# RGCN layer with a highway gate on one core: node orders at one visit, adding transfers behind the slot gathers, one branch flag, thin slots between full ones

## The chip, the cores and the metric

The kernel runs on one core of one Trainium2 chip. The metric is the device time of one execution in microseconds (us). The core's engines each have their own stream of instructions: TensorE (PE, matrix products; its loads of weights are listed as PEld), VectorE (DVE), ScalarE (ACT), GpSimd (POOL) and SyncE (SP). SP and POOL issue most transfers; the transfers themselves run on 16 DMA engines that all queues share. In the profile, queue q1 holds the transfers that SP issues and q0 those that POOL issues.

## The reference

The input is x of 1250 nodes by 1024 features, 20000 edges (src, dst, type), eight 1024 x 1024 relation matrices, a root matrix and a gate matrix of 2048 x 1024. All is fp32.

```python
h = relu(layernorm(x))
u = h @ root + bias
for r in range(8):
    mask = (edge_type == r)
    sums = segment_sum(h[src] * mask[:, None], dst)
    cnt = segment_sum(mask, dst)
    u = u + (sums / maximum(cnt, 1)[:, None]) @ weight[r]
z = concat([u, h], axis=1) @ w_gate + b_gate
out = x + (tanh(u) * z + h * (1 - z))
```

The mean over the edges of a relation and the product with its matrix may be exchanged: the kernel first forms y[r] = h @ weight[r] for all nodes, and then, for each destination node, adds rows of y with weight 1/cnt.

## The kernel before

**The steps.** PE works through eleven products in a row, called steps s = 0 to 10: seven of the relations and one before them, the root, the lower half of the gate matrix (applied to h) and last its upper half (applied to u). Nodes are cut into ND = 10 blocks of 128 (the last 98), which are taken in five pairs. Steps 1 to 9 save multiplications by a two-level scheme after Strassen and Winograd: each step has seven *kinds* n = 0 to 6, and (s, n) names one of them. A kind has five *calls* in which PE runs the products of one pair of blocks; between two calls a hook lets other work put its instructions into the streams. Where the text says "at (2,2), call 2" it means that hook. Steps 0 and 10 go by pairs of blocks, so (10, i) is pair i of the last step. Within a kind, PE's matmuls are the lines L330 and L337 (L589 in the last step), DVE adds to banks of partial sums (L438 in the first half of a kind, L461 near its end, L388, L381 and L382 for what goes to rows), ACT copies banks (L424, L448, L344 and others), DVE forms the next right factors (L238) and left factors (L276 to L286). Some left factors are loaded back from memory instead: L296, `w<-lefts_dram`, 512 KB each, issued by SP about twelve us before PE needs them.

**The order.** The kernel schedules itself by hand: what stands in an engine's stream is the order of the Python statements, and the generators below (`yield`) are moved on by one part at each call. So work beside the products lands at a fixed place in each engine's stream, and an engine that waits for one of its instructions holds up all that follows in its stream.

**The index part**, beside steps 0 to 2. It sorts the edges. Relations are taken in G = 3 groups (0 to 2, 3 to 5, 6 and 7). Within a group the nodes are ordered by how many edges they have, so block 0 of the order holds those with the most; K says how many slots (edges per node) each block needs: 21, 10, 8, 7, 7, 6, 5, 5, 4, 3 for groups 0 and 1, and 17, 7, 6, 5, 4, 4, 3, 3, 2, 2 for group 2. `nodes_in_order(g)` does ten one-hot matmuls (L804) from operands that DVE builds (L787 to L798), turns the result into node numbers, and issues ten gathers (helper `rows_of`, L728) of the edge lists, `idx<-table`, on POOL. It is called for groups 0, 1 and 2 at call 2 of (2,1), (2,2) and (2,3). Behind the gathers of each group stand 3, 3 and 4 adding transfers (L1237), `out<-h_dram` with accumulation, 512 KB each: the reference's `out = x + h + ...`. `counts(g)` (L769 to L774) counts the edges of each node and relation; `weights(g)` (L757 to L764) turns counts into `w_of`.

**The first branch.** If some node has more edges than the tables hold, `counts_over` does a long repair. It loads the flag `n_far` into a register on five engines and stands before step (3,0); all that is left of `counts` is done right before it. With these inputs the branch isn't taken, and each engine jumps over the body (some 280 instructions on DVE, 1400 on POOL, about 50 on the others).

**The groups.** From BEGIN = (3,1), `edges(g, ...)` goes through the slots of group g, one *visit* each: `add_slot` issues on POOL one gather of up to 128 rows of y (L1407, `got<-y,idx`, five buffers, 512 KB when all rows are in range; rows out of range move nothing) and has DVE multiply and add it (L1412) to the block's `u`. The visits are spread over the calls, 76 slots from (3,1) to (6,1) and from (6,1) to (8,5), and 53 from there on. `starts` and `leaves` give for each block the first visit and the one at which its `u` is done; groups 0 and 1 write `u` back to memory, and group 2 adds the root product (`hr_dram`) and goes on to the gate, where ACT takes tanh of it (L1857) and PE transposes it (L533).

**The second branch** stands after group 1: if nodes have more edges than K gives them slots, the remaining edges are added in a long body. Its flag `n_pass` comes from `passes_needed` (30 row maxima of `w_of`, L1498, and a chain of small operations, among them a transposition on PE). Before it stand `rest()` and `store_rows()`, which add and store the last rows of the step (L381, L382). It skips some 1220 instructions on DVE, 2060 on POOL, about 30 on ACT and PE.

**The last step.** `make_t1` to `make_t4` (L202, L206, L210, L214) form sums of the gate's right factors. `product` takes its pieces in the order of its small functions `p1()` to `p7()`; `p2` is the piece with A12.

## Time and profile before

| what | us |
|---|---|
| median of 3 runs | 1289.93 (1285.99 to 1290.58) |
| the profiled execution | 1283.34 |
| its span, first to last instruction | 1281.5 |
| PE busy | 1249.9 |
| DVE busy | 970.8 |
| POOL busy | 443.7 |
| ACT busy | 274.4 |
| mean granted clock of PE | 0.996 |

A row of the timeline has the start in us, the busy time, the engine, the line, the operation, output and inputs, the count, and in brackets the idle time before it with what ended it ("DVEq" is DVE's own sequencer, which includes branches). A row of the windows has the stretch, the busy time of each engine with the number of instructions, the granted clock, the share of the DMA engines in use and GB/s. Times are from the span's start.

### The profile page before, as it was taken

The numbers are of one execution on the slowest core, as the hardware profiler recorded it, in microseconds if no ns is written. First come the engines' busy times: TensorE is split into PE (matmuls) and PEld (weight loads), VectorE is DVE, ScalarE is ACT, GpSimd is POOL, SyncE is SP. The second block draws the span as 40 slices with busy tenths as digits, with TensorE's granted clock in tenths as the row PEclk, the third lists the DMA queues.
The fourth block names the chain that finished last, engine by engine and source line by source line (L and its number), as shares of the span: only waits on it lengthen the run. The fifth ranks groups of instructions, "written<-read, shape, count | busy, mean of one in ns | idle before, by whom it ended". The sixth has DMA issues, their size and how long they took to land.

```text
span 1281.5 us, 14045 instructions
## 1 busy us (share of the span) xinstructions
PE 1249.9 (98%) x4725; PEld 883.1 (69%) x4725; DVE 970.8 (76%) x1462; ACT 274.4 (21%) x517; POOL 443.7 (35%) x400
## 2 busy tenths in 40 slices
PE   9999999899989999999999999999999999999996
PEld 5444777677767777777777777777777777544443
DVE  7545898786579787887878779898888799766642
ACT  3452211121122112112111211211221121202210
POOL 1330000028202222322431333453442558854531
PEclk9999999999999999999999999999999999999999
DMA  7965445838946686898898768899995949999973
GB/s 303 195 191 163 156 149 195 242 107 211 294 149 224 205 280 222 321 335 305 287 341 281 251 197 294 294 331 352 365 301 204 349 141 342 346 333 228 234 150 57
DMA packets 130432, 317.87 MB, mean 248 GB/s; under 512 B 30999, under 2 KB 32222, under 8 KB 130190
## 3 DMA queue, kind: packets, MB, share of 16 engines
q1 hardware_dynamic: 85726, 186.64, 42.7%
q0 software_dynamic: 44336, 129.72, 34.3%
q8 instruction: 38, 0.62, 0.2%
q10 hardware_dynamic: 288, 0.52, 0.1%
q14 instruction: 44, 0.36, 0.1%
HBM read 258.79 MB, written 90.18 MB: 272 GB/s over the span
## 4 chain that ended last, share of the span: by engine, by line
PE 43%; issue 10%; DMA 7%; POOL 7%; DVE 2%; POOLq 0%; ACT 0%; DVEq 0%; SPq 0%; ACTq 0%
PE ps_n L330 14%; PE ps L330 14%; PE ps_b L337 9%; DMA got<-y,idx 5%; PE ps_q L330 4%; POOL got L1407 3%; DMA z_dram<-w 2%; PE ps_b L589 1%; POOL h_all L728 1%; POOL out_dram L739 1%; POOL u L728 1%; PE ps_n L589 1%; POOL w L728 0%; DVE h_all L1412 0%; DVE u L1412 0%
## 5 line engine op out<-in xcount | busy, mean ns | idle before, releaser
L1407 POOL DMA_INDIRECT got<-y,idx x205 | 256.0, 1249 | 435.5 <-DVE u L1412 332.6
L330 PE MATMUL ps<-w,h_all 128*128 128x256 f32 (+1 forms) x1040 | 258.7, 392 | 0.0
L1412 DVE SCALAR_TENSOR_TENSOR u<-got,w_of,u 128x1024 f32<-128x1024 f32 (+1 forms) x189 | 241.5, 1280 | 12.4 <-DMA got<-y,idx 9.8
L330 PE MATMUL ps_n<-w,w 128*128 128x256 f32 x976 | 234.2, 383 | 9.2 <-DVE ps L438 7.3
L330 PEld LDWEIGHTS ps_n<-w,w 128*128 128x128 f32 x976 | 185.0, 191 | 63.2 <-issue 22.2
L337 PE MATMUL ps_b<-w,h_all 128*128 128x512 f32 x504 | 226.6, 592 | 0.0
L330 PEld LDWEIGHTS ps<-w,h_all 128*128 128x128 f32 x1040 | 197.4, 190 | 39.6 <-issue 14.1
L337 PEld LDWEIGHTS ps_b<-w,h_all 128*128 128x128 f32 x504 | 95.8, 190 | 94.1 <-issue 90.9
L589 PE MATMUL ps_b<-w,h_all 128*128 128x512 f32 x312 | 139.4, 593 | 4.4 <-DVE w L206 2.6
L330 PE MATMUL ps_q<-w,w 128*128 128x256 f32 x488 | 116.8, 383 | 5.4 <-DMA w<-lefts_dram 5.4
L448 ACT COPY ps<-ps_n 128x512 f32<-128x512 f32 x122 | 64.8, 575 | 252.5 <-PE ps_n L330 209.1
L330 PE MATMUL ps<-w,w 128*128 128x256 f32 x488 | 115.6, 380 | 0.0
L330 PE MATMUL ps_n<-w,h_all 128*128 128x256 f32 x488 | 115.3, 379 | 0.0
L589 PEld LDWEIGHTS ps_b<-w,h_all 128*128 128x128 f32 x312 | 58.6, 190 | 77.4 <-issue 73.0
L438 DVE TENSOR_TENSOR ps<-ps_n,inner 128x256 f32<-128x256 f32 x122 | 50.5, 430 | 75.0 <-PE ps L330 67.8
L330 PEld LDWEIGHTS ps_q<-w,w 128*128 128x128 f32 x488 | 93.1, 191 | 19.4 <-DVE w L388 4.8
L330 PEld LDWEIGHTS ps<-w,w 128*128 128x128 f32 x488 | 93.1, 191 | 12.8
L330 PEld LDWEIGHTS ps_n<-w,h_all 128*128 128x128 f32 x488 | 92.7, 190 | 13.0 <-issue 0.5
L424 ACT COPY ps<-ps_n 128x256 f32<-128x256 f32 x122 | 39.7, 361 | 247.0 <-PE ps_n L330 178.6
L238 DVE TENSOR_TENSOR w<-w,w 128x2048 f32<-128x2048 f32 x36 | 82.3, 2287 | 0.3
L589 PE MATMUL ps<-w,h_all 128*128 128x512 f32 (+1 forms) x136 | 57.6, 567 | 0.0
L728 POOL DMA_INDIRECT idx<-table,node_key x30 | 32.5, 1082 | 58.6 <-DVE small L788 47.9
(247 smaller groups left out, 1154.8 us busy)
## 6 DMA issues: line engine op xcount, KB each, us to landing
w<-lefts_dram SPq DMA_DIRECT2D x102, 512.0 KB
w<-in_L_gnn_weight_dram SPq DMA_DIRECT2D x31, 1024.0 KB
y<-row SPq DMA_DIRECT2D x84, 256.0 KB
y<-w SPq DMA_DIRECT2D x42, 256.0 KB
w<-in_L_gnn_w_gate_dram SPq DMA_DIRECT2D x8, 1024.0 KB
lefts_dram<-w SPq DMA_DIRECT2D x14, 512.0 KB
h_dram<-h_all SPq DMA_DIRECT2D x9, 512.0 KB
y<-row SPq DMA_DIRECT2D x9, 512.0 KB
```

Of the source, the lines that this page charges most:

```text
L238: nc.vector.tensor_sub(w[to], w[a], w[b])
L330: nc.tensor.matmul(p, a[:, k], b[:, k], start=(fresh and k == 0), stop=(k == a.shape[1] - 1), skip_group_check=True)
L337: nc.tensor.matmul(to, h_op[NP - 1][:, ORDER[n], k], w[:, k], start=(fresh and k == 0), stop=(k == KQ - 1), skip_group_check=True)
L424: nc.scalar.copy(banks[2 * u][:, :H], xs[u])
L438: nc.vector.tensor_add(banks[2 * u][:, H:], xs[u], ys[:, u * H:(u + 1) * H])
L448: nc.scalar.copy(banks[2 * u + 1].rearrange("p (a n) -> p a n", a=2), xs[u][:, None, :].to_broadcast([P, 2, H]))
L589: nc.tensor.matmul(b[:, at], aop[:, i, k, :], w.of[i][:, k, at], start=(fresh and k == 0), stop=(k == KQ - 1), skip_group_check=True)
L728: nc.gpsimd.indirect_dma_start(out=to, out_offset=None, in_=of, in_offset=bass.IndirectOffsetOnAxis(ap=at, axis=0), compute_op=op)
L739: ins = nc.gpsimd.indirect_dma_start(out=of, out_offset=bass.IndirectOffsetOnAxis(ap=at, axis=0), in_=frm, in_offset=None, compute_op=op)
L1407: nc.gpsimd.indirect_dma_start(out=t[:n], out_offset=None, in_=y[g][:, :], in_offset=bass.IndirectOffsetOnAxis(ap=at[:n, d, k:k + 1], axis=0),
L1412: nc.vector.scalar_tensor_tensor(u[:n], t[:n], w, u[:n], op0=OP.mult, op1=OP.add)
```

## The change

- **Node orders.** `nodes_in_order` handles all three groups at one visit, call 2 of (2,2): the operands are built before it in parts, in separate tiles for each group, then thirty one-hot matmuls and thirty gathers in a row.
- **Adding transfers.** The ten L1237 transfers move into `beside_group` and stand on POOL behind all thirty gathers.
- **Counts.** `counts(0)` comes at (2,4), `counts(1)` and `counts(2)` at (2,5); each of them earlier in the program than step (3,0).
- **One flag.** `beyond()` finds from `idx` whether any block's next slot is in use, with a few comparisons for the blocks that share a K, and joins the answer with the other flag before the existing `any_over`, now at call 2 of (2,6). `passes_needed` and `n_pass` go. The register `far` serves both branches, so the second branch doesn't load one.
- **Branches.** The first now stands after (3,0), before (3,1); the second isn't preceded by `rest()` and `store_rows()`. Both get `preferred_fallthrough_block=False`: the path not taken falls into a short block that jumps over the body.
- **Slots.** Block 0's slots above K of block 1 (eleven in groups 0 and 1, ten in group 2, the thin ones) are put between the slots of the later blocks, one behind each of the first three of every four of these. Before, they came right after block 0's other slots. Block 0 of groups 0 and 1 now leaves at visit 43 instead of 29, of group 2 at 37 instead of 24.
- **Last steps.** `make_t1` moves to (5,3), `make_t2` to (6,1), `make_t3` to (6,2) of step 9, with other homes for t1 and t2; in a kind that is done in the regular way, part of the rows is put one call earlier; in the last `product`, `p2()` comes before `p7()`.

The tiles `pool_of`, `kpos`, `mid`, `found` and `held` are only allocated earlier, and `at` in `edges` lists the (block, slot) of each visit.

```diff
+    BESIDE = (4, 3)
...
-                self.place = dict(b11=old["a"], t3=old["e"], b22=old["b"], t1=old["d"],
-                                  t2=rights, b21=lefts, t4=old["c"])
+                self.place = dict(b11=old["a"], t3=old["e"], b22=old["b"], t1=rights,
+                                  t2=old["d"], b21=lefts, t4=old["c"])
...
+                if i == 3:
+                    to_rows_of(1, (0,))
...
-            to_rows_of(1)
+            to_rows_of(1, (2,))
...
+        elif (n, k) == (5, 3):
+            gate.make_t1()
         elif (n, k) == (6, 1):
-            gate.make_t1()
+            gate.make_t2()
         elif (n, k) == (6, 2):
-            gate.make_t2()
-        elif (n, k) == (6, 3):
             gate.make_t3()
...
         else:
+            p2()
             d = p7()
             last(d, 0)
             p3()
...
-    def nodes_in_order(g, pos, ids_f, a, b, small, many):
+    def nodes_in_order(pos, ids_f, room, many):
+        parts = []
+        for g in range(G):
+            a, b, small = room(g)
...
+            yield
...
+            parts.append((a, b, lo_f))
         while at_call[2] != 2:
             yield
-        p = sum_bank("ps_q")
-        for c in range(ND):
-            nc.tensor.matmul(p[:, :2 * ND], a[:, c], b[:, c], start=(c == 0), stop=(c == ND - 1))
...
-        for d in range(ND):
-            rows_of(idx[:, g, d, :], table_rows, node_key[:, g, d:d + 1])
+        p = sum_bank("ps_q")[:, :2 * G * ND].rearrange("p (g d) -> p g d", g=G)
+        for g, (a, b, lo_f) in enumerate(parts):
+            for c in range(ND):
+                nc.tensor.matmul(p[:, g], a[:, c], b[:, c], start=(c == 0), stop=(c == ND - 1))
...
+        for g in range(G):
+            for d in range(ND):
+                rows_of(idx[:, g, d, :], table_rows, node_key[:, g, d:d + 1])
+            yield
...
-                for g in range(G):
-                    yield from nodes_in_order(g, pos[:, g * ND:(g + 1) * ND], ids_f, junk, hot, room, many)
-                    assert not xh
-                    for d in range(g * ND // G, (g + 1) * ND // G):
-                        nc.gpsimd.dma_start(out[block(d)], h_dram[block(d)], accum_op=OP.add,
-                                            max_dma_last_dim=4 * D)
...
+                yield from nodes_in_order(pos, ids_f, room, many)
...
-            starts = [late + sum(K[g][:d]) for d in range(ND + 1)]
-            leaves = [starts[d + 1] - 1 + lag for d in blocks]
+            full = K[g][1]
+            thin = [(0, k) for k in range(full, K[g][0])]
+            at = [(0, k) for k in range(full)]
+            for j, a in enumerate((d, k) for d in blocks[1:] for k in range(K[g][d])):
+                at.append(a)
+                if j % BESIDE[0] < BESIDE[1] and thin:
+                    at.append(thin.pop(0))
+            starts = [late + at.index((d, 0)) for d in blocks]
+            leaves = [late + at.index((d, K[g][d] - 1)) + lag for d in blocks]
...
-        def passes_needed():
-            far_k = got()[:, :NHI]
-            nc.vector.memset(far_k, 0.0)
-            for g in range(G):
-                for d in range(ND):
-                    if K[g][d] < SLOTS:
-                        nc.vector.reduce_max(far_k[:, g * ND + d:g * ND + d + 1],
-                                             w_of[:, g, d, K[g][d]:], axis=AX.X)
...
         def beside_group():
-            yield
+            added = iter(range(ND))
+            def add_h():
+                for d in added:
+                    nc.gpsimd.dma_start(out[block(d)], h_dram[block(d)], accum_op=OP.add,
+                                        max_dma_last_dim=4 * D)
+                    return
             for g in range(G):
-                yield from counts(g)
+                for _ in range(3):
+                    yield
+                for _ in counts(g):
+                    add_h()
+                add_h()
+            yield
+            yield from beyond()
+            while at_call[2] != 2:
                 yield
+            any_over()
...
+        def beyond():
+            flags = const.tile([P, NHI], F32, name="flags")
...
+                    nc.vector.tensor_single_scalar(
+                        flags[:, used:used + n].rearrange("p (g d) -> p g d", d=e - d),
+                        idx[:, gs[0]:gs[-1] + 1, d:e, k], float(FAR), op=OP.is_lt)
...
+            nc.vector.reduce_max(most[:, 1:2], flags, axis=AX.X)
+            nc.vector.tensor_max(most[:, 2:3], most[:, 2:3], most[:, 1:2])
...
-            if (s, i) == (BEGIN[0], BEGIN[1] - 1):
-                for _ in ready:
-                    pass
-                counts_over()
-                ready = weights_of_groups()
+        assert next(ready, 0) == 0
+        far = load(n_far)
+        counts_over(far)
+        ready = weights_of_groups()
...
-        rest()
-        store_rows()
-        passes = nc.values_load(n_pass[0:1, 0:1], min_val=0, max_val=E // MORE,
-                                skip_runtime_bounds_check_because="no more passes than edges")
-        with tc.If(passes > 0):
+        with tc.If(far > 0, preferred_fallthrough_block=False):
```

More of the change, by code (lines that the diff above doesn't have):

```diff
@@ L1444, in edges @@
             for t in range(-1, leaves[-1] + 4):
-                for d in blocks:
-                    if starts[d] <= t < starts[d + 1]:
-                        add_slot(u[d], g, d, t - starts[d], idx[:, g], w_of[:, g])
+                if late <= t < late + len(at):
+                    d, k = at[t - late]
+                    add_slot(u[d], g, d, k, idx[:, g], w_of[:, g])
                 for d in blocks:
@@ L1746, in tile_rgcn_highway @@
             s, i = beside(group, sum(K[g]) + late + 1, s, i, CHANGE[g])
[L1749 to L1753 removed]
+        with tc.If(far > 0, preferred_fallthrough_block=False):
             def further(g, d, ks, at, w):
@@ L1768, in tile_rgcn_highway @@
                         further(g, d, range(K[g][d], SLOTS), idx[:, g], w_of[:, g])
-            over = nc.values_load(n_over[0:1, 0:1], min_val=0, max_val=E // MORE,
-                                  skip_runtime_bounds_check_because="no more passes than edges")
+            over = load(n_over)
             with tc.If(over > 0):
```

113 lines of the change are left out of this document (52 added, 61 removed).

## The prediction

> **What bounds the kernel now.** The page first: it says which engine fills the span.
>
> ```profile
> span 1281.5 us, 14045 instructions
> PE 1249.9 (98%) x4725; PEld 883.1 (69%) x4725; DVE 970.8 (76%) x1462; ACT 274.4 (21%) x517; POOL 443.7 (35%) x400
> ```
>
> TensorE (PE) is busy 98% of the span, so an edit pays only where it lets PE wait less. The change leaves PE's matmuls as they are in number and size. What can be won is the 31.6 us (1281.5 - 1249.9) in which PE stands still. The waits say who stood for whom: in total us, how often, the longest (four rows of PE, two of VectorE, DVE, for later):
>
> ```profile
> PE ps_n L330 <- DVE ps L438: 7.3, 4, 4.7
> PE ps_q L330 <- DMA w<-lefts_dram: 5.4, 3, 4.5
> PE ps_b L589 <- DVE w L206: 2.6, 1, 2.6
> PE ps_b L589 <- ACT row L639: 0.7, 1, 0.7
> DVE ps L438 <- PE ps L330: 67.8, 71, 4.4
> DVE h_all L1412 <- DMA got<-y,idx: 24.0, 9, 6.5
> ```
>
> Then the windows, to place those waits (start:end, length, busy time of PE, PEld, DVE, ACT, POOL with counts, granted clock, DMA share, GB/s):
>
> ```profile
> 240.00:280.00 40.00, 35.52 (x151) 27.55 (x150) 30.98 (x64) 9.68 (x21) 0.99 (x1) 0.96 0.48 162
> 360.00:400.00 40.00, 35.26 (x140) 27.36 (x140) 31.26 (x93) 9.17 (x19) 4.55 (x4) 0.96 0.49 163
> 960.00:1000.00 40.00, 38.86 (x157) 29.36 (x155) 31.38 (x50) 5.74 (x12) 11.62 (x13) 1.00 0.64 220
> 1080.00:1120.00 40.00, 37.93 (x139) 24.92 (x140) 30.89 (x40) 8.43 (x13) 32.76 (x24) 1.00 1.04 347
> 1120.00:1160.00 40.00, 37.41 (x99) 17.22 (x99) 25.67 (x24) 2.35 (x4) 18.25 (x12) 1.00 1.04 334
> ```
>
> Two stretches lose 4.5 us and more, and both show a granted clock of 0.96: one at 240 to 280, which the change doesn't touch, and one at 360 to 400, which holds the first branch. The others lose 1 to 3 us each, in the last stage, where the DMA engines are full (share 1.04).
>
> **The first branch (moved behind step (3,0)).** The timelines of PE and of DVE around it:
>
> ```profile
> 367.16 3.60 PE L337 MATMUL ps_b<-w,h_all 128*128 128x512 f32 x8
> 375.50 3.43 PE L330 MATMUL ps_n<-w,w 128*128 128x256 f32 x8 [4.74 <-DVE ps L438]
> 378.72 2.19 PE L330 MATMUL ps<-w,w 128*128 128x256 f32 x8
> 361.17 0.91 DVE L1386 MEMSET got<- 128x1024 f32 x1 [0.20 <-issue]
> 371.50 1.29 DVE L388 TENSOR_TENSOR w<-w,ps 128x512 f32<-128x512 f32 x2 [3.52 <-DVEq L1702]
> 374.71 0.73 DVE L438 TENSOR_TENSOR ps<-ps_n,inner 128x256 f32<-128x256 f32 x2
> 376.34 0.39 DVE L762 TENSOR_TENSOR w_of<-w_of,got 128x220 f32<-128x220 f32 x1
> ```
>
> From 361.17 to 367.98 DVE does the counts of groups 1 and 2, rushed because the branch stands there (the row at 361.17 is their first, and 3.52 us before 371.50 is their end). Then the jump costs it 3.52 us, and L388, L276, L277, L1401 and L1402 still stand ahead of L438, for which PE waits 4.74 us. PE then runs eight matmuls in 3.43 and eight in 2.19 us, where the quiet rows below have 1.89: 1.54 + 0.30 us more. The whole bill is 6.6 us.
>
> After the change the counts are done in steps (2,4) and (2,5), and DVE comes to the jump after L461 of (3,0). How the boundary between two steps runs without a branch is seen at 260 to 276:
>
> ```profile
> 264.70 0.80 DVE L461 TENSOR_TENSOR ps<-ps,inner 128x256 f32<-128x256 f32 x2
> 271.71 3.60 PE L337 MATMUL ps_b<-w,h_all 128*128 128x512 f32 x8
> ```
>
> L461 ends at 265.50, and the last matmuls that need no L438 end at 275.31: DVE has 9.8 us. What stands between is now the jump 3.52, then L276, L277, L1401 and L1402 (374.71 - 371.50 less the 1.2 of L388: 2.0), the first weights (376.73 - 375.44, L438's end to L762's: 1.3) and L438 (0.73): 7.6 us, 2.2 to spare. So the stall goes: -6.6. Bounds: 0 (the whole bill is paid at the new place) to -6.6; I take -6.6 because the spare is over half the jump. The false side now falls into a short block that jumps over the body, where before the compare itself jumped; the skipped body is the same, so the jump is priced at the same 3.52. The Trainium skill ("Runtime: NRT & Kernel Launch", Instruction fetch mechanics) says that a taken branch whose target lies outside the fetched window has to fetch it before going on; that speaks against any gain from the new block order, and by it the moved branch still pays 3.5, which the sum has already. The trace agrees with 3.52 on DVE, while PE shows no wait on its own queue there.
>
> The flags from `idx` (some twenty short DVE operations) replace the row maxima, DVE work on both sides; PE waits for DVE at none of those places, and DVE stood idle 67.8 us before L438 over the run, so 0. If that cover is gone, 20 operations of 0.39 us (the small one at 376.34, an upper bound) are 8 us late once.
>
> **The adding transfers (L1237).** Before, 3, 3 and 4 of them stand behind each ten slot gathers; after, all 10 follow the thirtieth. The windows of that stretch, POOL's rows and PE's at the loads of left factors:
>
> ```profile
> 296.09 1.13 POOL L728 DMA_INDIRECT idx<-table,node_key  x1 [0.30 <-DVE b L794]
> 320.94 0.94 POOL L728 DMA_INDIRECT idx<-table,node_key  x1 [0.30 <-issue]
> 327.60 3.59 POOL L1237 DMA_DIRECT2D out_dram<-h_dram  x4
> 330.00:340.00 10.00, 10.00 (x40) 7.23 (x39) 4.64 (x10) 1.22 (x3) 1.19 (x2) 1.00 1.06 251
> 340.00:350.00 10.00, 9.62 (x45) 8.17 (x44) 6.16 (x13) 2.29 (x5) 0.00 (x0) 1.00 1.04 350
> 350.00:360.00 10.00, 10.00 (x40) 7.31 (x39) 6.83 (x16) 1.65 (x3) 0.00 (x0) 1.00 0.64 245
> 360.00:370.00 10.00, 10.00 (x41) 7.62 (x41) 6.16 (x18) 1.22 (x3) 0.00 (x0) 1.00 0.47 152
> 346.39 1.97 PE L330 MATMUL ps_q<-w,w 128*128 128x256 f32 x8 [0.38 <-DMA w<-lefts_dram]
> 350.11 0.32 SPq L296 DMA_DIRECT2D w<-lefts_dram  x1
> 249.11 3.27 PE L330 MATMUL ps_q<-w,w 128*128 128x256 f32 x8 [4.48 <-DMA w<-lefts_dram]
> ```
>
> A gather takes POOL 1.25 us (0.94 + 0.30). The visit stays in (2,2), where group 1's gathers now begin (296.09), so thirty end near 296 + 30 x 1.25 = 334, and the ten transfers start there instead of 293, 310 and 328. Behind the four issued at 327.60 the engines are full at 251 GB/s from 330 to 340, and reach 350 GB/s from 340 to 350, mostly without them; PE waited 0.38 us for a load. So the four took 10.6 - 251 x 10 / 350 = 3.4 us of the engines beyond what their bytes cost at the full rate (2 MB at 350 GB/s: 5.7), 9 in all. Ten take 2.5 times that, 23 us. Free engine time from 334 to 370, with the four gone, is 3.6 + 5.3 in the last two windows, 9 from the four, and some 3 before new gathers fill it: 21. So it all but fits, but not in order: while the ten are served, SP's loads get under half, and the load issued at 350.11, which had 12 us, stands behind some 5 us of backlog. Bounds: 0.4 (the row at 346.39) to 4.48 + (3.27 - 1.89) = 5.9 for each of two loads, 11.8. I take one such stall, 5, because the demand of SP's loads falls by half after 360. By the Trainium skill ("DMA: Bandwidth & Descriptors", Arbitration) an engine takes turns between its rings packet by packet; that rule leaves SP its turn, so it speaks for the lower end.
>
> **The second branch.** Without a fresh load of the flag, and with the last adds and stores of a step behind it instead of ahead:
>
> ```profile
> 994.99 0.21 DVE L1812 TENSOR_SCALAR piece_at<-node 128x1 int32<-128x1 int32 x2 [1.63 <-DVEq L1753]
> 995.08 1.01 POOL L728 DMA_INDIRECT u<-u_dram,node  x1 [8.38 <-DVEq L1753]
> 1000.01 1.99 PE L330 MATMUL ps_n<-w,w 128*128 128x256 f32 x8 [1.16 <-DVE ps L438]
> ```
>
> Four of the adds L381 and L382 (the shape of L388, 0.6 each) no longer stand ahead of DVE's jump: it comes 2.4 us earlier, more than PE's 1.16, which go. -1.2; bounds -1.2 and +1.2 (the adds, now behind the jump, are in L438's way). POOL's first gather of group 2 starts some 3 us earlier.
>
> **The slot order.** Thin slots (few rows in range) now stand between full ones. Windows in group 2, and the first uses of its block 0:
>
> ```profile
> 1005.00:1025.00 20.00, 19.44 (x83) 15.32 (x82) 18.68 (x28) 3.50 (x8) 9.84 (x9) 1.00 0.99 372
> 1025.00:1045.00 20.00, 20.00 (x85) 15.72 (x84) 18.16 (x21) 7.39 (x15) 7.90 (x5) 1.00 0.23 65
> 1065.00:1085.00 20.00, 18.81 (x79) 14.41 (x78) 19.58 (x26) 4.01 (x8) 16.37 (x12) 1.00 1.02 331
> 1101.94 2.09 ACT L1857 ACTIVATE h_all<-u 128x1024 f32<-128x1024 f32 x2
> 1113.08 0.60 PE L533 MATMUL ps_n<-ident,u 128*128 128x128 f32 x4
> ```
>
> The thin stretch moves 65 GB/s, then the engines are full until 1160: spread out, that idle share takes up later load, and DVE's waits for gathers shrink. PE loses 2.07 of 40 us at 1080 to 1120 and 1.19 of 20 at 1065 to 1085; I take half of it, -1.5. Bounds: -3 to +14: block 0 leaves at visit 37 instead of 24 of 65. By the list of calls that is in kind (9,4), and its last add stands at about 1090 (an estimate from the pace of the kinds); ACT takes it at 1101.94, 11 us later.
>
> **The last steps.** DVE L206 (t2) ran late behind a multiply-add that waited for its gather (the 2.6 above). It now stands ahead of it: -2.6; bounds -2.6 to 0 (the wait passes to t3). The piece A12 taken before p7 gives ACT L639 its time: -0.7, bounds -0.7 to +0.7. The tail behind the last matmul stays.
>
> **The sum:** -6.6 + 5 - 1.2 - 1.5 - 2.6 - 0.7 = -7.6 us. The profiled execution took 1283.34 us (span 1281.5), 6.6 under the median of the three timed runs, 1289.93. So 1275.7 in such an execution, and 1282.3 beside the median: 1282, 0.6% faster. 0.5% (6.4 us) is about what a measurement of this kernel can tell from no change.
>
> **Rivals.**
> - The transfers cost twice what I took: two loads of left factors come late, each with over 4 us of waiting and cold matmuls behind it, +11.8. Sum -0.8: 1289. For it speaks 249.11, where one late load did just that; against it the 0.38 at 346.39 with four transfers. It decides from 3 us of lateness on for the load issued at 350.11.
> - The jump moves but its cost stays: at the new place DVE, or ACT, whose copies L424 stand behind the same jump, comes over 2.2 us later than worked out, and PE waits 4 us again. Sum about -2: 1288. Against it: the rush of counts, 6.8 us, is gone from in front of it.
> - Slower: block 0 of group 2 is late. If its gathers fall behind by more than the 11 us between 1090 and 1101.94, ACT's L1857 waits, and PE's turning at 1113.08 behind it, with the engines full until 1160 and no matmuls left to bring forward: at the upper bound +14, with -1.5 not won, sum +7.9: 1298. For it: DVE's gathers waited up to 6.5 us each in that stretch; against it: the earlier start.
>
> The Trainium skill ("TensorE: Matmul & The Clock Gate", Part 1) has the clock fall after about 3.4 us without work; the 3.43 us of eight matmuls behind a 4.74 us wait agree. By it two waits of 2.5 us would cost 5 and one of 5 us 6.5 to 7, which changes a term by under 2.
>
> **How the numbers follow.** Forecast 0.46; transfers twice as dear 0.18; jump stays 0.12; block 0 late 0.14; several loads starved, or block 0 and loads together, 0.10 (to 1305). Faster by over 0.5%: the forecast's upper part with 0.44; same: the rest of it and the two middle rivals, 0.32; slower 0.24. The lower end is the sum with the transfers at 0.4 and the slot order at -3, -13.7 with the rest as taken: 1276, less 3 for the spread of the runs: 1273. The upper is the slower rival's 1298. Below lies 0.08, above 0.12.
>
> **What would show it.** PE's wait for L438 after the branch gone, and 360 to 400 near 40 us: step one. Waits for `lefts_dram` between 345 and 385: the transfers' bill; none there would make the gain larger. No wait for L206 and L639 in the last steps. Wrong is it if ACT's L1857 or PE's L533 wait for `u`, or if the branch's stall returns at 385.

## The result, and the profile after

The changed kernel is slower: 1305.2 us median of five runs (1301.73 to 1308.64) beside 1287.81 for the kernel before (1285.99 to 1290.58), a ratio of 1.0136 with a 95% interval of 1.0107 to 1.0165. The prediction was 1282, faster by 0.6%, with 1273 to 1298 as its range. The profiled execution of the changed kernel took 1308.64 us.

Lines have moved: L331 and L338 are the matmuls that were L330 and L337, L441 and L464 the adds that were L438 and L461, L383 was L382, L1401 and L1406 the gather of y and its multiply-add, L1509 the adding transfers, L615 was L612. The head of the page, and the waits of PE (in total us, how often, the longest):

```profile
span 1306.9 us, 14007 instructions
PE 1259.2 (96%) x4724; PEld 888.5 (68%) x4724; DVE 968.1 (74%) x1443; ACT 273.9 (21%) x517; POOL 434.1 (33%) x400
```

```profile
PE ps_q L331 <- DMA w<-lefts_dram: 15.6, 3, 7.9
PE ps_n L331 <- DVE ps L441: 6.4, 5, 3.5
PE ps L331 <- DVE row L383: 4.6, 1, 4.6
PE ps_q L331 <- DVE u L1406: 2.4, 1, 2.4
PE ps_b L592 <- ACT row L615: 1.8, 1, 1.8
```

PE now stands still for 47.7 us (1306.9 - 1259.2) instead of 31.6. Waits for loads of left factors went from 5.4 to 15.6 us. The wait for L206 is gone, and so is the one for L639. Waits for L383 and L1406 are new. The windows say where:

```profile
320.00:360.00 40.00, 31.73 (x125) 24.08 (x124) 25.94 (x63) 3.97 (x9) 19.52 (x22) 0.90 0.81 194
360.00:400.00 40.00, 38.33 (x153) 29.47 (x152) 18.08 (x40) 10.17 (x21) 3.15 (x3) 0.97 0.77 242
900.00:940.00 40.00, 37.58 (x151) 29.47 (x150) 30.99 (x39) 8.58 (x18) 16.01 (x14) 0.96 0.90 336
1000.00:1040.00 40.00, 36.53 (x147) 28.51 (x146) 30.11 (x46) 5.44 (x12) 15.68 (x15) 0.96 0.80 288
1040.00:1080.00 40.00, 36.31 (x143) 27.90 (x142) 33.39 (x41) 10.29 (x22) 19.48 (x13) 0.96 0.57 194
1120.00:1160.00 40.00, 35.37 (x100) 17.99 (x99) 25.20 (x29) 6.13 (x8) 29.02 (x21) 0.91 1.05 330
```

360 to 400, where the first branch cost 4.7 us of PE, loses 1.7 now (before: 35.26 busy, after: 38.33), and that is a wait for a load at 370; the branch has moved on to 397, and PE waits 1.35 us behind it at 403. But 320 to 360 loses 8.3, and four stretches from 900 on lose 2.4 to 4.6 each. In all six the granted clock is below 1.

The largest loss stands behind the adding transfers. The timelines of POOL, SP and PE, and the windows:

```profile
334.23 6.90 POOL L1509 DMA_DIRECT2D out_dram<-h_dram  x8
...
337.31 0.32 SPq L297 DMA_DIRECT2D w<-lefts_dram  x1
...
357.21 3.75 PE L331 MATMUL ps_q<-w,w 128*128 128x256 f32 x8 [7.87 <-DMA w<-lefts_dram]
```

```profile
340.00:350.00 10.00, 9.34 (x38) 6.84 (x36) 8.77 (x22) 1.68 (x4) 2.87 (x4) 1.00 1.06 249
350.00:360.00 10.00, 2.79 (x7) 2.28 (x8) 3.54 (x14) 0.01 (x1) 0.00 (x0) 0.61 1.06 254
360.00:370.00 10.00, 8.72 (x28) 5.62 (x26) 2.83 (x16) 1.17 (x2) 0.00 (x0) 0.88 1.06 258
```

The transfers start at 334.23, as forecast. From 340 to 370 the DMA engines are full at 249 to 258 GB/s. The load that SP issued at 337.31, three us behind the first transfer, is there at 357.21, 19.9 us later. PE waits 7.87 us for it and then runs cold (eight matmuls in 3.75 us).

The queues in the stretch from 340 to 370 (packets, MB, share of the time of the 16 engines; q0 is POOL's, q1 SP's):

```profile
q0 software_dynamic: 1268, 4.57, 76.7%
q1 hardware_dynamic: 1314, 3.01, 29.2%
```

Both queues got nearly the same number of packets through, 1268 and 1314, but POOL's held the engines 2.7 times as long. By the trace's single packets, 4 KB of an adding transfer took 0.33 us, 4 KB of SP's 0.17 and 2 KB of SP's 0.10. So SP's loads and stores together had 29% of the engines' time, and the load had to share that with SP's own weight load of 1 MB, issued at 335.24.

The second branch, on DVE, POOL and PE:

```profile
1004.31 0.75 DVE L464 TENSOR_TENSOR ps<-ps,inner 128x256 f32<-128x256 f32 x2
1010.68 0.21 DVE L1822 TENSOR_SCALAR piece_at<-node 128x1 int32<-128x1 int32 x2 [5.62 <-issue]
...
1012.15 1.00 POOL L731 DMA_INDIRECT u<-u_dram,node  x1 [11.36 <-DVE row L383]
...
1016.42 2.53 PE L331 MATMUL ps_n<-w,w 128*128 128x256 f32 x8 [3.47 <-DVE ps L441]
```

DVE stands idle 5.62 us at the jump, where it was 1.63 and 1.59 around it before, and POOL's first gather of group 2 starts 1.5 us behind DVE's L1822 (before: 0.1 behind L1812), not earlier. And the last stage, on DVE, PE and ACT:

```profile
1130.88 1.28 DVE L1406 SCALAR_TENSOR_TENSOR u<-got,w_of,u 128x1024 f32<-128x1024 f32 x1 [3.32 <-DMA got<-y,idx]
1132.08 1.27 DVE L383 TENSOR_TENSOR row<-w,ps 128x512 f32<-128x512 f32 x2
...
1132.81 9.30 PE L331 MATMUL ps<-w,h_all 128*128 128x512 f32 x16 [4.63 <-DVE row L383]
...
1130.21 2.00 ACT L1867 ACTIVATE h_all<-u 128x1024 f32<-128x1024 f32 x2
```

DVE's L383, which frees a bank for PE, stands in the stream behind multiply-adds that wait for their gathers (3.32 us the last of them). ACT's tanh of block 0 (L1867, 1130.21) isn't among PE's waits.

### The profile page after: what moved, and what is told of

It is laid out like the page before. It is cut to its first block, busy times and chain, and to the rows that moved or that the text cites. A ratio compares the mean times of both kernels' runs of the same rounds, so it can differ in the third digit from the quotient of the medians.

```text
span 1306.9 us, 14007 instructions
## 1 busy us (share of the span) xinstructions
PE 1259.2 (96%) x4724; PEld 888.5 (68%) x4724; DVE 968.1 (74%) x1443; ACT 273.9 (21%) x517; POOL 434.1 (33%) x400
## 5 line engine op out<-in xcount | busy, mean ns | idle before, releaser
L1401 POOL DMA_INDIRECT got<-y,idx x205 | 251.3, 1226 | 448.1 <-DVE u L1406 347.1
L331 PE MATMUL ps<-w,h_all 128*128 128x256 f32 (+1 forms) x1040 | 260.9, 394 | 4.6 <-DVE row L383 4.6
L1406 DVE SCALAR_TENSOR_TENSOR u<-got,w_of,u 128x1024 f32<-128x1024 f32 (+1 forms) x189 | 240.7, 1277 | 18.2 <-DMA got<-y,idx 17.9
L331 PE MATMUL ps_n<-w,w 128*128 128x256 f32 x976 | 235.8, 385 | 9.3 <-DVE ps L441 6.4
L331 PEld LDWEIGHTS ps_n<-w,w 128*128 128x128 f32 x976 | 187.1, 193 | 65.2 <-issue 22.2
L331 PEld LDWEIGHTS ps<-w,h_all 128*128 128x128 f32 x1040 | 198.2, 191 | 45.9 <-issue 15.2
L338 PE MATMUL ps_b<-w,h_all 128*128 128x512 f32 x504 | 226.7, 592 | 0.0
L338 PEld LDWEIGHTS ps_b<-w,h_all 128*128 128x128 f32 x504 | 95.7, 190 | 94.3 <-issue 90.9
L331 PE MATMUL ps_q<-w,w 128*128 128x256 f32 x488 | 121.1, 393 | 18.0 <-DMA w<-lefts_dram 15.6
L441 DVE TENSOR_TENSOR ps<-ps_n,inner 128x256 f32<-128x256 f32 x122 | 50.3, 428 | 95.1 <-PE ps L331 93.6
L331 PEld LDWEIGHTS ps_q<-w,w 128*128 128x128 f32 x488 | 95.5, 197 | 33.1 <-issue 8.2
L331 PE MATMUL ps<-w,w 128*128 128x256 f32 x488 | 116.5, 382 | 0.0
L331 PE MATMUL ps_n<-w,h_all 128*128 128x256 f32 x488 | 115.3, 379 | 0.0
L331 PEld LDWEIGHTS ps<-w,w 128*128 128x128 f32 x488 | 93.7, 192 | 13.1
L331 PEld LDWEIGHTS ps_n<-w,h_all 128*128 128x128 f32 x488 | 92.7, 190 | 13.0 <-issue 0.5
L731 POOL DMA_INDIRECT idx<-table,node_key x30 | 29.4, 980 | 71.5 <-DVE node L814 62.7
```

The costliest lines, as they stand in the source:

```text
L331: nc.tensor.matmul(p, a[:, k], b[:, k], start=(fresh and k == 0), stop=(k == a.shape[1] - 1), skip_group_check=True)
L338: nc.tensor.matmul(to, h_op[NP - 1][:, ORDER[n], k], w[:, k], start=(fresh and k == 0), stop=(k == KQ - 1), skip_group_check=True)
L441: nc.vector.tensor_add(banks[2 * u][:, H:], xs[u], ys[:, u * H:(u + 1) * H])
L731: nc.gpsimd.indirect_dma_start(out=to, out_offset=None, in_=of, in_offset=bass.IndirectOffsetOnAxis(ap=at, axis=0), compute_op=op)
L1401: nc.gpsimd.indirect_dma_start(out=t[:n], out_offset=None, in_=y[g][:, :], in_offset=bass.IndirectOffsetOnAxis(ap=at[:n, d, k:k + 1], axis=0),
L1406: nc.vector.scalar_tensor_tensor(u[:n], t[:n], w, u[:n], op0=OP.mult, op1=OP.add)
```

## The experiments

All ratios are to the kernel before, run beside each of them, with the 95% interval. They aren't quotients of the medians, from which they differ by up to 0.15%; us beside a ratio are its distance from 1 times 1288 us. Names with b_ are the kernel before with one part of the change done, names with a_ the changed kernel with parts taken back.

### One part at a time, in the kernel before

**b_acc**: only the adding transfers moved.

```diff
                 for g in range(G):
                     yield from nodes_in_order(g, ...)
-                    for d in range(g * ND // G, (g + 1) * ND // G):
-                        nc.gpsimd.dma_start(out[block(d)], h_dram[block(d)], accum_op=OP.add, ...)
+                for d in range(ND):
+                    nc.gpsimd.dma_start(out[block(d)], h_dram[block(d)], accum_op=OP.add, ...)
```

> The kernel before, with the ten adding transfers behind the thirtieth slot gather (its gathers stay at three visits). Theory of the transfers (from the trace of after: PE waits 7.9 us for a load of left factors between 349 and 357, and 320 to 360 loses 10.3 instead of 0.6 us): 7 to 11 us slower than before, ratio 1.006 to 1.008, with one wait of over 5 us for lefts_dram within 20 us of the first transfer. Rival (the wait of after comes from the gathers of all groups at one visit, not from the transfers): within 2 us of before, no such wait.

Measured: 1.0091 (1.0058 to 1.0125), 11.7 us. The timeline of its PE:

```profile
359.35 3.75 PE L330 MATMUL ps_q<-w,w 128*128 128x256 f32 x8 [11.28 <-DMA w<-lefts_dram]
```

The theory holds, a little above its upper end: the burst alone makes PE wait over 11 us for one load, with the slot gathers at their three old visits.

**b_form**: only the form of the two branches.

```diff
-            with tc.If(load(n_far) > 0):
+            with tc.If(load(n_far) > 0, preferred_fallthrough_block=False):
...
-        with tc.If(passes > 0):
+        with tc.If(passes > 0, preferred_fallthrough_block=False):
```

> The kernel before, with only the form of the two branches changed (the path not taken falls into a short block that jumps over the body). Theory (form is dearer: in after DVE stands idle 5.5 and 5.6 us at the two branches, before 3.5 and 1.6): DVE's idle time grows by 2 at the first and up to 4 us at the second branch and the time by 3 to 6 us, ratio 1.002 to 1.005. Rival (the longer idle time comes from what stands ahead of the branches in after, not from the form): idle times as before within 0.5 us, time within 1 us.

Measured: 1.0046 (1.0030 to 1.0062), 6 us. DVE and PE at its second branch:

```profile
1000.33 0.21 DVE L1812 TENSOR_SCALAR piece_at<-node 128x1 int32<-128x1 int32 x2 [3.62 <-issue]
1005.61 0.69 DVE L277 TENSOR_TENSOR w<-w,w 128x512 f32<-128x512 f32 x1 [4.47 <-issue]
...
1008.24 3.49 PE L330 MATMUL ps_n<-w,w 128*128 128x256 f32 x8 [6.03 <-DVE ps L438]
```

At the second branch DVE's idle times are 3.62 and 4.47 us instead of 1.63 and 1.59, and PE's wait behind it is 6.03 instead of 1.16. At the first branch DVE's idle time was 3.83 instead of 3.52 and PE's wait 5.05 instead of 4.74, so in this kernel the form costs hardly anything there, against the theory. DVE's sequencer at the second branch (count, ns, first and last start), in the kernel before and then in b_form:

```profile
L1753 DVEq EVENT_SEMAPHORE  x2: 21/21/21, 994.8 to 994.9; - x2
L1753 DVEq COMPARE_BRANCH  x1: 63/63/63, 991.7 to 991.7; - x1
```

```profile
L1753 DVEq COMPARE_BRANCH  x2: 47/54/61, 995.0 to 997.0; - x2
L1753 DVEq EVENT_SEMAPHORE  x2: 21/21/21, 996.7 to 996.9; - x2
```

Before, the one branch is taken at 991.7, while DVE still adds until 993.36, and the sequencer goes on some 3 us later, at 994.8: part of the 3 us runs beside work. In b_form the first branch, at 995.0, leads into the short block; there the two semaphore events stand at 996.7 and 996.9, when DVE's last add (L382) has ended at 996.70, and only then comes the jump, at 997.0. DVE goes on 3.3 us behind it, with nothing to do meanwhile. That explains the growth from 1.63 to 3.62; why the second idle time grew from 1.59 to 4.47 stays open. The Trainium skill ("Runtime: NRT & Kernel Launch", Instruction fetch mechanics) says that a taken branch to code outside the fetched window stalls until it is fetched. Some 3 us behind the jump stand in both forms; that they are this fetch no run here shows.

**b_slot**: only the order of the slots (the lines of `edges` in the diff above).

> The kernel before, with only the order of the slots changed (thin ones between full ones). Theory (the order costs: in after, waits at 922, 1040 and 1127 that before has not, 4 + 6 + 7 us, stand where full gathers now run side by side with the loads of left factors): 8 to 16 us slower, ratio 1.006 to 1.012, with waits for lefts_dram or behind L1412 in 900 to 1140. Rival 1 (those waits come from the dearer second branch, which delays group 2): under 2 us slower. Rival 2 (the prediction's): 1.5 us faster.

Measured: 1.0030 (1.0011 to 1.0048), 3.9 us, between the theory and its rivals; that it gains is refuted. The window of 1020 to 1040 in the kernel before, then in b_slot, and two new waits of PE in b_slot (its lines from L331 on are those of before plus one):

```profile
1020.00:1040.00 20.00, 20.00 (x87) 16.10 (x86) 18.16 (x22) 5.47 (x12) 7.92 (x6) 1.00 0.41 132
```

```profile
1020.00:1040.00 20.00, 17.48 (x66) 13.27 (x65) 15.38 (x19) 2.90 (x7) 7.00 (x6) 0.91 0.72 275
```

```profile
1027.34 2.45 PE L331 MATMUL ps_q<-w,w 128*128 128x256 f32 x8 [2.52 <-DMA w<-lefts_dram]
...
1115.46 2.84 PE L331 MATMUL ps<-w,h_all 128*128 128x512 f32 x6 [3.43 <-DVE row L383]
```

Before, the thin slots left the DMA engines more than half idle at 1020 to 1040, and PE ran without a wait. With full gathers in that stretch a load of left factors comes 2.5 us late. At 1115 DVE comes to L383 late, behind multiply-adds that wait for their gathers. So the idle share wasn't free to take: SP's loads came on time in it.

**b_move**: only the first branch moved behind step (3,0), with what is left of the counts.

```diff
             s, i = next(steps)
-            if (s, i) == (BEGIN[0], BEGIN[1] - 1):
-                for _ in ready:
-                    pass
-                counts_over()
-                ready = weights_of_groups()
+        for _ in ready:
+            pass
+        counts_over()
+        ready = weights_of_groups()
```

> The kernel before, with only the first branch (and the counts that are left) moved behind step (3,0). Theory of the prediction: PE's wait of 4.7 us for L438 and the cold matmuls behind it go, 5 to 7 us faster, ratio 0.9945 to 0.996. Rival (the wait moves along with the branch): 0 to 2 us faster, with a wait of 3 us or more for L438 at about 385.

Measured: 0.9967 (0.9955 to 0.9979), 4.2 us faster. PE and DVE at the branch:

```profile
386.38 3.60 PE L337 MATMUL ps_b<-w,h_all 128*128 128x512 f32 x8
389.87 1.99 PE L330 MATMUL ps_n<-w,w 128*128 128x256 f32 x8
...
385.82 0.20 DVE L1401 TENSOR_SCALAR rcp<-rcp 128x80 f32<-128x80 f32 x1 [3.52 <-DVEq L1702]
...
389.06 0.76 DVE L438 TENSOR_TENSOR ps<-ps_n,inner 128x256 f32<-128x256 f32 x2
```

The jump costs DVE the same 3.52 us, L438 ends at 389.82, and PE goes on at 389.87 without a wait. The stall is gone, though the gain (2.7 to 5.8 us by the interval) is a little under the theory's 5 to 7. There is next to nothing to spare.

**b_twice**: the branch stays where it was; two parts of the counts are done at each call.

```diff
         def on(j):
             next(ready, None)
+            next(ready, None)
```

> The kernel before, with two parts of the counts done at each call instead of one, so that nothing of them is left at the first branch, which keeps its place before (3,0). Theory (the jump alone, 3.5 us, fits into DVE's slack at a boundary, and the rush of counts made the stall): as b_move, 4 to 6 us faster, ratio 0.9955 to 0.997. Rival (the place matters, because behind it L388, which the boundary before (3,1) has not, stands ahead of L438): 1 to 3 us faster, PE still waits 2 us or more for L438 at 370.

Measured: 0.9986 (0.9972 to 0.9999). The counts moved earlier, though not wholly: 0.8 us of them are left between L461 and the jump, where 6.8 us stood. DVE there:

```profile
371.05 1.28 DVE L388 TENSOR_TENSOR w<-w,ps 128x512 f32<-128x512 f32 x2 [3.52 <-DVEq L1702]
...
375.68 0.76 DVE L438 TENSOR_TENSOR ps<-ps_n,inner 128x256 f32<-128x256 f32 x2
```

PE still waits 1.8 us for L438, close to the rival's 2 us, and the ratio fits the rival (1 to 3 us). So the rush was part of the stall, and the place another: before (3,0) L388 (1.28 us) also stands between the jump and L438, behind (3,0) it doesn't. All else that stands there, with the same 0.8 us of counts ahead of the jump, b_move has too, and it has no wait.

### Parts taken back from the changed kernel

**a_three**: the transfers back behind each ten gathers, branches in the old form, slots in the old order. `behind(g)` issues group g's share of the transfers.

```diff
             for d in range(ND):
                 rows_of(idx[:, g, d, :], table_rows, node_key[:, g, d:d + 1])
+            behind(g)
             yield
...
-            with tc.If(far > 0, preferred_fallthrough_block=False):
+            with tc.If(far > 0):
```

> The changed kernel with three parts taken back: the adding transfers stand 3, 3 and 4 behind each ten gathers, the branches have their old form, the slots their old order. Theory (these three hold all the loss, and the moved branch, the order of t1 to t3 and of A12 do gain): 6 to 10 us faster than before, ratio 0.992 to 0.995, with no wait of PE over 1.5 us at the first branch. Rival (something else in the change costs too, such as the counts or the flags in steps 2): not faster than before.

Measured: 0.9913 (0.9881 to 0.9946), a median of 1279.2 us: faster than both kernels. Its window of the transfers, and DVE at its second branch:

```profile
320.00:360.00 40.00, 39.89 (x162) 30.25 (x161) 28.26 (x80) 5.78 (x12) 20.56 (x22) 1.00 1.02 275
```

```profile
989.48 0.22 DVE L1821 TENSOR_SCALAR piece_at<-node 128x1 int32<-128x1 int32 x2 [0.77 <-DVEq L1763]
```

With the engines as full as ever at 320 to 360 (1.02), PE loses 0.1 us: the same ten transfers, in threes and fours between the gathers, do not starve SP's loads. At the first branch PE waits 0.29 us. The second branch costs DVE 0.77 us with the register already loaded and the old form.

**a_form**, **a_slot** and **a_acc**: only the form, only the order, only the transfers taken back.

> The changed kernel with only the form of the branches taken back. Theory (the parts add up but for some 5 us; the form alone cost the kernel before 6 us): 6 to 9 us faster than the changed kernel, so 8 to 11 slower than before, ratio 1.006 to 1.009, with DVE's idle time at the second branch about 1 instead of 5.6 us. Rival (in the changed kernel other waits take the place of this one): under 2 us faster than the changed kernel, ratio 1.012 or more.

> The changed kernel with only the slots in their old order. Theory (the waits at 922, 1040 and 1127 are the order's): 9 to 13 us faster than the changed kernel, so 4 to 8 slower than before, ratio 1.003 to 1.006, and these three waits gone. Rival (the order alone cost the kernel before 4 us, and the other 7 belong to the dearer second branch): 4 us faster than the changed kernel, ratio 1.010, the wait at 922 gone and those behind the branch still there.

> The changed kernel with only the adding transfers put back, 3, 3 and 4 behind each ten gathers. Theory: the wait of 7.9 us for lefts_dram at 349 and the cold matmuls behind it go, 10 to 12 us faster than the changed kernel, so 5 to 7 slower than before, ratio 1.004 to 1.006. Rival (the transfers of after cost nothing that the earlier ones would not cost elsewhere): waits for lefts_dram of the same sum between 300 and 350.

Measured: a_form 1.0208 (1.0179 to 1.0237), a_slot 1.0238 (1.0212 to 1.0264), a_acc 1.0022 (1.0006 to 1.0039). a_acc is as expected and a little better. The two others are *slower* than the changed kernel, which no theory had. The windows of a_form, and ACT, DVE and PE there:

```profile
305.00:315.00 10.00, 7.24 (x23) 4.44 (x22) 2.15 (x4) 0.00 (x0) 7.56 (x9) 0.93 0.27 62
315.00:325.00 10.00, 2.98 (x9) 2.05 (x8) 0.00 (x0) 0.59 (x1) 7.56 (x9) 0.67 0.13 9
325.00:335.00 10.00, 0.00 (x0) 0.00 (x0) 0.00 (x0) 0.00 (x0) 8.17 (x11) 0.50 0.16 12
```

```profile
323.31 0.59 ACT L352 COPY w<-ps_b 128x512 f32<-128x512 f32 x1 [19.13 <-remote]
...
337.40 1.28 DVE L379 TENSOR_TENSOR w<-row,ps 128x512 f32<-128x512 f32 x2 [23.56 <-remote]
...
338.00 3.45 PE L331 MATMUL ps<-w,h_all 128*128 128x256 f32 x8 [20.02 <-ACT ps L451]
```

From 318 to 338, while POOL issues the rest of its thirty gathers (to 332.8) and the first adding transfers, PE stands still for 20 us. ACT and DVE wait for something that the profile calls "remote"; the DMA engines are nearly idle (share 0.13 and 0.16). The semaphores that L352 and L379 wait on are those of SP's loads of 297.8 and 306.5. a_slot shows the same wait of 20.0 us. In both kernels PE goes on 5.2 us after the first adding transfer.

**a_two**: form and order both taken back, the transfers left behind the thirty gathers.

> The changed kernel with the branches in their old form and the slots in their old order; the adding transfers stay behind all thirty gathers. a_form and a_slot each had a wait of PE of 20 us near 318 that the changed kernel has not, while POOL issues the thirty gathers and ACT and DVE wait for loads whose data had moved. Theory 1 (the thirty gathers in a row together with the ten transfers behind them can hold back the end of SP's loads, in some builds and not in others): either 2 to 5 us slower than before (without it) or 20 to 25 us slower (with it). Theory 2 (the 20 us come from the form or the order that was taken back): here both are, so the wait is there, ratio 1.016 to 1.02.

Measured: 1.0039 (1.0023 to 1.0054), without the 20 us: PE's longest wait for a load is 7.0 us. So neither the form nor the order brings those 20 us by itself: with both as in the changed kernel, or both taken back, they are absent.

**a_late**: as a_two, the transfers spread over the visits of group 0.

```diff
+                if g == 0 and t >= 10 and t % 6 == 4 and t // 6 <= ND:
+                    b = t // 6 - 1
+                    nc.gpsimd.dma_start(out[block(b)], h_dram[block(b)], accum_op=OP.add, ...)
```

> As a_two, with the ten adding transfers moved further back: one at every sixth slot visit of group 0 from the tenth on, on POOL between the gathers of y. If the burst of ten is what cost 12 us, and thirty gathers in a row cost nothing by themselves: 8 to 11 us faster than before, ratio 0.9915 to 0.994, the same as a_three. If thirty gathers in a row hold back SP's loads without the transfers behind them: the wait of 20 us near 318 is there, 10 us slower than before.

Measured: 1.0005 (0.9991 to 1.0018), neither: some 12 us slower than a_three, although its transfers are spread out. There is no wait at 318, and none at 350; but beside the gathers of y, with the engines full (1.01 to 1.07 from 570 to 590), a load is late in its turn. SP issued it at 572.61, 0.3 us behind one of the transfers, and it came 16.4 us later:

```profile
588.99 3.32 PE L331 MATMUL ps_q<-w,w 128*128 128x256 f32 x7 [4.35 <-DMA w<-lefts_dram]
```

That wait and the cold matmuls behind it are about half of the 12 us; the rest isn't followed here.

**a_last**: as a_three, with the last steps (t1 to t3, rows of the regular kind, A12) as before.

> As a_three (all three dear parts taken back), with the last steps as before too: places and order of t1 to t3, the rows of the regular kind, A12 behind p7. Theory of the prediction: 3 us slower than a_three, so 6 faster than before, ratio 0.9945 to 0.996, with PE's waits for L206 (2.6 us) and L639 (0.7) back. Rival (other waits had taken their place in a_three, ACT L615 3.1 and DVE L574 2.1 us): within 1 us of a_three.

Measured: 0.9930 (0.9910 to 0.9951), 2.2 us behind a_three by the ratios and 1.3 by the medians, which the intervals don't tell apart. PE's waits in a_last, then in a_three:

```profile
PE ps_b L590 <- DVE w L207: 2.8, 1, 2.8
```

```profile
PE ps_b L592 <- ACT row L615: 3.1, 1, 3.1
```

The wait for the sum t2 (L207 in a_last) goes in a_three, as forecast, and in its place PE waits 3.1 us for ACT's L615, 16 us on. The waits are the rival's; the times don't decide.

### The 20 us

**n_form** and **n_after**: a_form and the changed kernel with six tiny memsets on DVE ahead of the thirty gathers. **n_none**: a_form without the ten adding transfers, so its output lacks h.

```diff
+        for _ in range(6):
+            nc.vector.memset(parts[0][2], 0.0)
         for g, (a, b, lo_f) in enumerate(parts):
             nc.vector.tensor_copy(lo_f, p[:, g, :ND])
```

> As a_form, with six tiny DVE memsets (some 0.5 us) ahead of the thirty gathers. If the wait of 20 us near 318 hangs on how gathers and loads happen to meet: it goes or changes, the time falls to about 1.010 of before or less. If it belongs to the program as such (old form, all transfers behind): it stays, 1.018 to 1.023.

> The changed kernel with the same six memsets. If the wait of 20 us hangs on how gathers and loads meet: it may show here, 1.02 to 1.035 of before; or stay away, 1.012 to 1.016. If the form or the slots decide it: it stays away.

> As a_form, with the ten adding transfers left out (the output lacks h). If the transfers behind the gathers take part in the wait of 20 us: it is gone, and the time is 8 to 12 us over a_three's slot order cost, 0.995 to 1.002 of before. If the thirty gathers in a row alone do it: the wait near 318 is there, 1.012 to 1.018.

Measured: n_form 1.0096 (1.0067 to 1.0126), n_after 1.0151 (1.0113 to 1.0189), n_none 0.9966 (0.9947 to 0.9985). None has a wait of 20 us. With 0.75 us of other work (the six memsets) a_form loses it, which speaks for a chance of how gathers and loads meet. But the chip changed too: a_form and a_slot ran on chip 4 of the record, a_two on chip 1, the three n_ kernels on chip 3, and for the changed kernel the record names none, so that the wait belongs to a chip isn't excluded. The two kernels that showed it have all thirty gathers in a row with nothing of POOL's between them; none of the kernels that keep transfers among the gathers showed it. What holds the loads' semaphores back stays open: that n_none lacks it proves nothing, as n_form lacks it too.

n_form and n_after also give the form of the branches in the changed kernel, side by side and with nothing else different: 0.55%, 7.1 us (two runs of each). At the first branch DVE is idle 4.08 us in n_form and 5.67 in n_after, and PE's wait behind it is none and 3.14; at the second 0.88 and 5.82, and PE's wait none and 3.68.

n_none's window of 320 to 360 says what the transfers cost otherwise:

```profile
320.00:360.00 40.00, 39.63 (x161) 29.97 (x160) 29.94 (x81) 6.20 (x13) 9.99 (x11) 1.00 0.61 192
```

Without them the engines are 0.61 busy and PE loses 0.4 us. n_form beside n_none is 1.30% slower, 16.7 us (14.8 by the medians).

### The account

Four kernels that differ in one part each (n_form's memsets aside) make a chain. Differences are of ratios, times 1288 us:

| kernel | ratio | what is added | us |
|---|---|---|---|
| a_three | 0.9913 | moved branch, one flag, last steps, one visit of orders | -11.2 |
| a_two | 1.0039 | transfers behind the thirty gathers | +16.2 |
| n_form | 1.0096 | thin slots between full ones | +7.3 |
| changed kernel | 1.0136 | form of the branches | +5.2 |

Each difference is uncertain by some 4 to 5 us, the last one by as much as itself; n_after beside n_form puts the form at 7.1. Alone in the kernel before, the three dear parts cost 11.7, 3.9 and 6, 21.6 in sum, and 28.7 in the chain: by these numbers the burst and the order cost more in the tighter kernel, but the intervals overlap.

Beside the sum of the prediction: the three dear parts are 25.2 us above it (16.2 for 5, 7.3 for -1.5, 5.2 for 0), which is the whole miss. Its other four terms come to -11.1, and a_three measures -11.2. That agreement is partly luck, as the parts below show.

## Why the prediction was wrong, point by point

- **The first branch (-6.6).** The mechanism was right, and b_move has it in its rows. It was worth 4.2 us alone. The working gave 2.2 us to spare; b_move shows 0.05 (389.82 against 389.87). Nor did the jump keep its 3.52 us everywhere: in the old form DVE was idle 3.92 us there in a_two and 5.91 in a_three, and why isn't shown. In the changed kernel it is 5.53, and PE still waits 1.35 us; by n_form, which has no such wait, that is the form's.
- **The adding transfers (+5).** This step failed by its size: 11.7 us alone and 16.2 in the chain. The sum of engine time came close: full to about 370, as worked out. The wrong choice was to take one stall of 5 us near the load of 350.11, because "the demand of SP's loads falls by half after 360". The load that suffers is the one issued at 337, right behind the transfers, not one that meets their end; it took 19.9 us, and PE ran cold after it. The first rival had the size (11.8), but from two late loads where the runs show one very late. The packet rule of the Trainium skill ("DMA: Bandwidth & Descriptors", Arbitration) was read as speaking for the lower end. The trace agrees with the turns, 1268 packets of q0 to 1314 of q1; what the reading left out is how long a turn lasts: the adding packets took 0.33 us, SP's 0.10 to 0.17, so that SP's queue had 29% of the time and its load didn't get its 512 KB within the twelve us it had.
- **The form of the branches (0).** This failed outright: "the skipped body is the same, so the jump is priced at the same 3.52". The body is the same; that DVE's earlier work has to end in the block ahead of the jump was not priced. The form cost 6 us alone, of which this wait is some 2 (b_form, 1.63 to 3.62); the rest stays open. The second branch's -1.2 was right with the old form (a_three: 0.77 us of DVE, and no wait of PE there) and turned into a wait of 3.47 us with the new one.
- **The slot order (-1.5).** Wrong in sign: +3.9 alone, +7.3 in the chain. The words "that idle share takes up later load" counted the DMA engines' time, not who needs it when. Full gathers in the thin stretch made a load late there (b_slot, 2.52 us), and the later stretch got no lighter for PE, whose wait there (3.43) came from DVE's place in line behind gathers. The third rival had the sign, but not its mechanism: ACT's L1857 (L1867 after) and the turning were not what PE waited for; the late load and L383 behind L1406 were.
- **The last steps (-3.3).** L206 and L639 did vanish from PE's waits. The gain was 1.3 to 2.2 us, within the intervals: ACT's L615 took the place.
- **The second rival (the jump's cost stays).** It didn't decide: PE's wait there was 1.35 us instead of 4.74.
- **The clock.** The cold matmuls cost a little more than the sums had: eight took 3.75 us behind the waits of 7.87 and 11.28 us, where the sums had 3.43 and 3.27. The clock also fell behind waits shorter than the 3.4 us that the prediction goes by: after the wait of 2.52 us in b_slot eight matmuls took 2.45 us, where unhindered ones take 1.89, and the granted clock of that window is 0.91.

The rest of a_three's 11.2 us beyond branch (4.2) and last steps (1.3 to 2.2) is some 5 us, hardly more than the uncertainty of a_three itself (4 us either way), and no run takes it apart: the second branch, the flag that replaces the row maxima, and the orders at one visit.

## What to carry to other kernels

A mean share of the DMA engines doesn't say whether a load comes in time: a_three ran 320 to 360 at 1.02 and PE lost 0.1 us, the changed kernel at 0.81 and lost 8.3. What counted here is what stood in the queues between a load's issue and its need, twelve us later. So idle share beside PE's loads isn't capacity to give away by the sum: a burst of background transfers, or full gathers moved into a quiet stretch, is paid by the next load behind them. Nor is spreading enough by itself: transfers in threes and fours among the small gathers cost nothing to speak of (a_three), but with one at a time among full gathers of y a load came late again, right behind one of them (a_late). Ask of each transfer which load is issued just after it. Price the form of a branch, not only the code it skips, and measure bundled parts one by one: here parts worth -11 us were buried under +29.

## What was not expected of the hardware

- The same not-taken branch cost DVE 0.88 us (n_form) or 5.82 us (n_after), by which block it falls into; the two kernels differ in nothing else.
- Ten adding transfers of 512 KB in a row held all DMA engines at 249 to 258 GB/s from 340 to 370 and let one load of 512 KB take 19.9 us: the two queues got nearly equal numbers of packets through, but a 4 KB packet took 0.33 us in an adding transfer and 0.17 in a plain one. The same ten, 3, 3 and 4 between gathers, cost PE under 1 us from 280 to 400 (a_three).
- With thirty gathers in a row on POOL, two builds out of the six shown that have the transfers right behind them (after, a_form, a_slot, a_two, n_form, n_after) had ACT and DVE wait some 20 us for loads while the DMA engines were nearly idle; it was absent with 0.75 us of work ahead, on another chip. Its cause is open.
